# Graph sums and experts on one core: where the weights' bf16 parts are cast, and which engine adds the rows' bias

## Chip, cores and metric

One Trainium2 chip, one core of it. The metric is the device time of one execution in microseconds (us). Before the change: 493.82 us, the median of 3 runs (492.48 to 494.44).

## The reference, cut to what matters

There are 2048 nodes with 256 features each, 67,584 edges whose list is sorted by `dst`, and 8 experts.

```python
x = x + segment_sum(edge_weight[:, None] * layernorm(x)[dst], src) + node_vec1   # graph step
x = x + moe(layernorm(x)[None])                                                  # top 2 of 8 experts, gelu
```

`node_vec1` has one value per node, so it is a bias of the rows of x. The change lies in the graph step. The experts' part (router, lists of rows, slots of 256 rows that run two matmul layers) is untouched.

## The kernel before, in words

**Stage 1, the graph step**, takes the first 200 us or so. The sparse matrix of edge weights is built as dense column blocks and multiplied with the normalised x, called `xn_sb` (128 rows of nodes per partition block, 16 blocks b; 256 features and 8 router columns each). The result is added onto `acc`, which holds x from the start.

The matrix is built in 32 steps n (L472 on, `NH = 2 * NB`). One step makes 64 columns:

- For every fourth step a quarter q of the column pairs is prepared: GpSimd (POOL) gathers a run of `dst` (`get_run`, L215), ScalarE (ACT) counts how many lie before (`count_before`, L227, a Sign activation with a sum), VectorE (DVE) turns the count into a place (`get_at`), and POOL gathers windows of 128 edges (`get_win`, L240: source, destination, weight). `keys_of` (DVE, L271 to L275) makes keys of them. `turn_keys` transposes keys and weights on TensorE (PE, L283 and L284) and ACT casts them (L288, L291).
- Weights are fp32, and one-hots are multiplied in bf16. So each weight is split in three bf16 parts: part 0 is cast in `turn_keys`, parts 1 and 2 in `next_part(q, 1)` and `next_part(q, 2)`. Each subtracts the part before from the rest on DVE (L302) and casts the new rest on ACT (L303) into `w2`.
- `make_hots(n)` makes on DVE the one-hots `hl` (L313, 128x4096 bf16) and `eq` (L318), and multiplies `eq` with the weight parts into `hr`: parts 0 and 1 on DVE (L325, 128x2048), part 2 on POOL (L325, 128x1024). POOL's product is made to wait for DVE's. `ahead` and `between` are calls that are issued in between. The constant `iota_t` that `hl` and `eq` compare with lies in PSUM.
- `make_cols(n)` multiplies `hr` with `hl` on PE (L348, 96 matmuls). ACT copies the sums out of PSUM (L351), SP writes them to DRAM (`ad`, L352) and reads the step before back as columns (`ac`, L359).
- From n = 8 on, `dense` (PE, L366) multiplies finished column blocks with `xn_sb` for two row blocks at a time, in groups of 3, 3, 3, 3 and 4 column blocks; `add` (DVE) adds the sum onto `acc` one step later. The list `late` holds what is still to add.

The order of every engine is written out by hand (`tc.manual_schedule`), so an instruction that waits holds back all behind it on its engine. In each step the order is: hots of n + 1, gathers, late adds, columns of n, sums, keys turned, and then the `if n < ...` blocks.

**What the change touches.** Step 0 is prepared ahead of the loop. Its `make_hots(0, ...)` has `ahead=part_1`, which issues `next_part(0, 1)` and then `keep_x(3)`. `keep_x(i)` is an ACT copy of 128x1024 fp32 (L413) that takes the fourth transposed quarter of x (`turn_x(3)`, PE, L406) out of PSUM. `next_part(0, 2)` follows between `eq` and `hr`. So on ACT the order is: cast of part 1, copy of x, cast of part 2, then `sd` (Sqrt, L459) and `count_before(2)` (L227). `scale_x` (DVE, L465 and L466, `rs` and `shift` of 128x16) needs `sd`.

The first group of sums (8 adds, two row blocks each) also adds the bias: `add(..., first=True)` runs two `scalar_tensor_tensor` (L376, 128x256, PSUM + bias + acc) and one small `tensor_add` for the router columns (L378). All later adds are one `tensor_add` of 128x528 (L373).

Of the kernel before, what the change touches and what calls it, by code (L numbers as in the profile page):

```python
# [13 lines left out]
AF = mybir.ActivationFunctionType  # L14
OP = mybir.AluOpType
# [11 lines left out]
def kernel(  # L27
# [30 lines left out]
    nc = tc.nc  # L58
    N, D = x.shape
    NE, _, H = W1.shape  # L60
    E = src.shape[0]
    NB = N // P
# [18 lines left out]
    DX = D + NE  # L81
# [20 lines left out]
    acc = consts.tile([P, NB, DX], F32, name="acc")  # L102
# [110 lines left out]
    def get_run(q):  # L213
        runs[q] = find.tile([P, EJ], I32, name="run", bufs=3)
        nc.gpsimd.indirect_dma_start(  # L215
            out=runs[q],
            out_offset=None,
            in_=dst.rearrange("(p j) -> p j", p=P),
            in_offset=bass.IndirectOffsetOnAxis(ap=blk_i[:, q:q + 1], axis=0),
        )  # L220
# [4 lines left out]
    def count_before(q):  # L225
        sign = find.tile([P, EJ], BF16, name="sign")
        nc.scalar.activation(sign, runs[q], AF.Sign, bias=colp[:, q:q + 1], scale=-1.0,  # L227
                             accum_out=at[:, q:q + 1])
# [69 lines left out]
    def next_part(q, i):  # L298

        k2, w2, rest = parts[q]  # L300
        r = prep.tile([P, P], F32, name=f"r{i}")
        nc.vector.tensor_tensor(by_half(r), by_half(rest), w2[:, :, i - 1, :, 0], OP.subtract)  # L302
        nc.scalar.copy(w2[:, :, i], by_half(r)[..., None].to_broadcast([P, P // GH, GH, 2]))  # L303
        parts[q] = (k2, w2, r)

    def make_hots(n, *between, ahead=None):

        k2, w2, _ = parts[n // 4]  # L310
        g = n % 4
        hl = hotl.tile([P, GH, P], BF16, name="hl")
        nc.vector.tensor_tensor(hl.rearrange("p g (n t) -> p g n t", t=2),  # L313
                                two(k2[:, 0], g, P), pair(P), OP.is_equal)
        if ahead:
            ahead()
        eq = hotr.tile([P, GH, RK], BF16, name="eq")
        nc.vector.tensor_tensor(eq.rearrange("p g (n t) -> p g n t", t=2),  # L318
                                two(k2[:, 1], g, RK), pair(RK), OP.is_equal)
        for b in between:  # L320
            b()
        hr = hotr.tile([P, 3, GH, RK], BF16, name="hr")

        def times(engine, i0, i1):
            return engine.tensor_tensor(  # L325
                hr[:, i0:i1].rearrange("p i g (n t) -> p (i g) n t", t=2),
                eq[:, None, :, :].to_broadcast([P, i1 - i0, GH, RK]),
                w2[:, g, i0:i1].rearrange("p i g t -> p (i g) t")[:, :, None, :]
                .to_broadcast([P, (i1 - i0) * GH, RK // 2, 2]), OP.mult)

        v = times(nc.vector, 0, 2)
        third = times(nc.gpsimd, 2, 3)
        tc.add_manual_dep(third.ins, v.ins.name, WAITS, reason="beside one-hots of rows")
        return hl, hr
# [26 lines left out]
    def dense(cbs, b):  # L361

        pa = ps_s.tile([P, 2, 512], F32, name="py1")
        for i in range(2):
            for c in cbs:
                nc.tensor.matmul(pa[:, i, :DX], acs[c][:, b + i, :], xn_sb[:, c, :],  # L366
                                 start=(c == cbs[0]), stop=(c == cbs[-1]))
        return b, pa, cbs[0] == 0

    def add(b, pa, first=False):  # L370

        if not first:
            nc.vector.tensor_add(acc[:, b:b + 2, :], acc[:, b:b + 2, :], pa[:, :, :DX])  # L373
            return
        for i in range(2):
            nc.vector.scalar_tensor_tensor(acc[:, b + i, :D], pa[:, i, :D], nv_c[:, b + i:b + i + 1],  # L376
                                           acc[:, b + i, :D], op0=OP.add, op1=OP.add)
        nc.vector.tensor_add(acc[:, b:b + 2, D:], acc[:, b:b + 2, D:], pa[:, :, D:DX])  # L378

    ads, acs = {}, {}  # L380
    ET = mybir.EngineType
# [1 line left out]
    with tc.manual_schedule(engines=ALL):  # L383
        first = find.tile([P, 1], F32, name="first")
# [25 lines left out]
        def keep_x(i):  # L410
            pt = xTs[i]
            xTs[i] = rowsp.tile([P, GH // QP, P], F32, name="ar")
            nc.scalar.copy(xTs[i], pt)  # L413
# [17 lines left out]
        for _ in range(3):  # L431
            get_win(0)
        nc.vector.scalar_tensor_tensor(wc, ws[:, None, :].to_broadcast([P, KD, NE]), -1.0 / D,
                                       wr_sb, op0=OP.mult, op1=OP.add)
# [13 lines left out]
        weigh_x(1)  # L448
        turn_x(3)

        def part_1():
            next_part(0, 1)
            keep_x(3)

        hots = {0: make_hots(0, lambda: next_part(0, 2), ahead=part_1)}
        get_run(3)
        block_stats(bn, mv, acc, range(15, NB))
        sd = small.tile([P, NB], F32, name="sd", bufs=1)
        nc.scalar.activation(sd, mv[:, :, 1], AF.Sqrt, bias=eps_sb, scale=1.0)  # L459
        count_before(2)  # L460
        rs = small.tile([P, NB], F32, name="rs", bufs=1)
        shift = small.tile([P, NB], F32, name="shift", bufs=1)

# [8 lines left out]
        for n in range(NH):  # L472
# [30 lines left out]
            for p in late:  # L503
                add(*p)
# [6 lines left out]
            while len(todo) > NB // 2 and (budget >= len(todo[0][0]) or n == NH - 1):  # L511
                cbs, b = todo.pop(0)
                budget -= len(cbs)
                if len(late) == 2:
                    add(*late.pop(0))
                late.append(dense(cbs, b))
# [9 lines left out]
            if n < 4:  # L526
                for b in range(4 * n, 4 * n + 4):
                    nc.scalar.activation(xn_sb[:, b, :D], acc[:, b, :D], AF.Identity,
                                         bias=shift[:, b:b + 1], scale=rs[:, b:b + 1])
            if n == 1:  # L530

                tr = ps_a.tile([P, 4, P], F32, name="pa").rearrange("p a b -> p (a b)")
                nt = NE * KH + 2 * NE * KD + NB
                cols = consts.tile([P, nt], F32, name="cols")
                o = 0
                for rows in (b1_rows, g_rows, be_rows, nv_rows):
                    m = rows.shape[0]
                    nc.tensor.transpose(tr[:, o:o + m], rows, ident[:m, :m])
                    o += m
                nc.scalar.copy(cols, tr[:, :nt])  # L540
                nv_c = cols[:, NE * (KH + 2 * KD):]
# [8 lines left out]
            if n == 8:  # L550
# [3 lines left out]
                                               op1=OP.subtract)  # L554
# [12 lines left out]
        for p in late:  # L567
            add(*p)
# [9 lines left out]
    with tc.If(n_used < E):  # L578
        nc.sync.dma_start(xn_d.rearrange("(b p) d -> p b d", p=P), xn_sb)
        nc.sync.dma_start(acc[:, :, :D], xv)  # L580
        for b in range(NB):
            nc.vector.tensor_scalar(acc[:, b, :D], acc[:, b, :D], nv_c[:, b:b + 1], None,
                                    op0=OP.add)
# [6 lines left out]
        with tc.tile_pool(name="any", bufs=2) as anyp, tc.tile_pool(  # L590
# [5 lines left out]
            with tc.For_i(0, E // P, 1) as t:  # L596
# [18 lines left out]
                for b in range(NB):  # L615
                    hot = anyp.tile([P, P], F32, name="hot")
                    nc.vector.tensor_scalar(hot, iota_p, s_b[:, b:b + 1], w_t, op0=OP.is_equal,
                                            op1=OP.mult)
# [53 lines left out]
    with tc.manual_schedule(engines=ALL - {ET.Pool}):  # L672
# [526 lines left out]
        for p in range(2):  # L1199
            late.append(dense(groups[-1], 2 * p))  # L1200

        def finish(p, more=True):

            add(*late.pop(0))
            if more and p + 2 < NP:
                late.append(dense(groups[-1], 2 * p + 4))
            square(2 * p)
            square(2 * p + 1)
# [148 lines left out]
```

## Time and profile before

| | |
|---|---|
| median of 3 runs | 493.82 us (492.48 to 494.44) |
| the profiled execution, its own time | 489.82 us |
| its span, first to last instruction | 488.1 us |
| granted TensorE clock, mean | 0.958 |
| busy, share of the span | PE 92%, PEld 78%, DVE 57%, ACT 37%, POOL 39% |
| ACT `L413` copy of 128x1024 | 0.99 to 1.01 us |
| ACT `L303` cast of a weight part | 0.41 us |
| ACT `L528` scaling of 128x256, four in a row | 2.06 to 2.08 us |
| DVE `L376` with two instructions, then `L378` | 0.87 us, 0.16 us |
| DVE `L373` | 0.70 us |

How to read it: busy PE time is that of pipelined matmuls whose ends are modelled. A row of the timeline has start and duration in us, engine, line, operation, what it writes and reads, and in brackets the idle time of its engine before it and what ended it. An instruction on DVE or ACT can start some 0.1 us before the one ahead has ended, so the pace of a chain is read from start to start.

### The profile page before, as it was taken

Reading aid. Unit: us, or ns where it says so; the run is one execution under the profiler, and the core shown is the slowest. Engines: PE = TensorE matmul, PEld = TensorE weight load, DVE = VectorE, ACT = ScalarE, POOL = GpSimd, SP = SyncE. Lnnn points to the kernel's source line nnn. Section 1 sums busy time; section 2 is a strip of 40 time slices with the busy share of each in tenths; the row PEclk is TensorE's granted clock in tenths of the full one; section 3 lists DMA queues with packets and bytes.
Section 4 is the critical chain, followed back from the end, with each engine's and each line's share of the span. In section 5 each row is a group of like instructions: output and inputs, shape, how many; then the busy total and the mean of one; then the engine's idle time right before and its main releaser. Section 6 shows DMA issues by size and latency. Waiting matters only on the chain. (4 is left out here: it accounts for less than half of the span.)

```text
span 488.1 us, 12137 instructions
## 1 busy us (share of the span) xinstructions
PE 447.8 (92%) x4972; PEld 379.7 (78%) x4972; DVE 276.6 (57%) x643; ACT 178.6 (37%) x408; POOL 191.1 (39%) x157
## 2 busy tenths in 40 slices
PE   4876588999999989899999999999999999999992
PEld 3765466887887878788888888888877778888882
DVE  7999999999999972217849322321434231221111
ACT  2476734243242210027483433223331333322330
POOL 3577674455543430000132644333452333622331
PEclk9575879999999999999999999999999999999998
DMA  7228999989799599933532898998897747822520
GB/s 222 55 79 214 263 274 284 254 210 248 185 230 240 133 239 263 361 124 109 179 105 45 260 355 239 348 343 259 280 351 226 240 116 217 220 60 47 175 73 23
DMA packets 83252, 99.38 MB, mean 204 GB/s; under 512 B 8800, under 2 KB 73872, under 8 KB 81072
## 3 DMA queue, kind: packets, MB, share of 16 engines
q1 hardware_dynamic: 74000, 84.03, 58.0%
q0 software_dynamic: 7712, 13.38, 12.2%
q10 hardware_dynamic: 1472, 1.06, 0.7%
q8 instruction: 43, 0.70, 0.6%
q14 instruction: 25, 0.20, 0.1%
HBM read 72.61 MB, written 27.94 MB: 206 GB/s over the span
## 5 line engine op out<-in xcount | busy, mean ns | idle before, releaser
L366 PE MATMUL py<-xn_sb,ac 128*128 128x264 f32 x512 | 122.0, 394 | 2.7 <-DVEq L578 1.4
L1047 PE MATMUL ph<-xeT,w 128*128 128x256 f32 x512 | 114.7, 381 | 1.7 <-PEq L1304 1.0
L1061 PE MATMUL py<-w,hT 128*128 128x256 f32 x512 | 114.3, 381 | 0.0
L366 PEld LDWEIGHTS py<-xn_sb,ac 128*128 128x128 f32 x512 | 95.8, 191 | 21.3 <-issue 4.1
L1047 PEld LDWEIGHTS ph<-xeT,w 128*128 128x128 f32 x512 | 96.8, 190 | 16.2 <-issue 1.7
L1061 PEld LDWEIGHTS py<-w,hT 128*128 128x128 f32 x512 | 96.0, 190 | 13.0 <-issue 0.8
L1049 ACT ACTIVATE hT<-ph,ec 128x256 f32<-128x256 f32 x128 | 60.4, 473 | 106.0 <-PE ph L1047 55.9
L325 POOL TENSOR_TENSOR hr<-eq,w 128x1024 bf16<-128x1024 bf16 x32 | 61.2, 1912 | 73.5 <-DVE hr L325 58.9
L1069 POOL DMA_INDIRECT y_d<-ys,to_i x28 | 45.3, 1619 | 89.9 <-DVE ys L1064 56.1
L313 DVE TENSOR_TENSOR hl<-k,iota_t 128x4096 bf16<-128x4096 bf16 x32 | 72.9, 2279 | 0.0
L348 PE MATMUL pa<-hl,hr 128*32 128x128 bf16 x3072 | 58.0, 234 | 15.3 <-POOL hr L325 8.4
L348 PEld LDWEIGHTS <-hr 128*32 128x32 bf16 x3072 | 49.0, 104 | 27.0 <-issue 12.8
L973 POOL DMA_INDIRECT xs<-xr_d,to_i x36 | 37.5, 1043 | 67.3 <-DVE z L712 40.1
L351 ACT COPY ar<-pa 128x512 f32<-128x512 f32 x64 | 36.4, 583 | 49.0 <-PE pa L348 42.3
L1021 DVE TENSOR_SCALAR xeT<-px,ec 128x256 f32<-128x256 f32 x34 | 16.9, 539 | 64.7 <-PE px L1012 63.9
L1064 DVE SCALAR_TENSOR_TENSOR ys<-py,wt,b2w 128x256 f32<-128x256 f32 x32 | 15.3, 484 | 64.6 <-PE py L1061 48.9
L325 DVE TENSOR_TENSOR hr<-eq,w 128x2048 bf16<-128x2048 bf16 x32 | 39.1, 1223 | 0.6
L373 DVE TENSOR_TENSOR acc<-acc,py 128x528 f32<-128x528 f32 x32 | 22.2, 700 | 28.7 <-PE py L366 28.7
L1036 ACT ACTIVATE b2w<-b,wt 128x256 f32<-128x256 f32 x34 | 15.3, 499 | 33.5 <-DVE wt L1034 31.3
L318 DVE TENSOR_TENSOR eq<-k,iota_t 128x1024 bf16<-128x1024 bf16 x32 | 21.8, 681 | 0.0
L680 ACT ACTIVATE sq<-acc,less_m 128x256 f32<-128x256 f32 x16 | 8.0, 498 | 32.7 <-DVE acc L373 32.7
L303 ACT CAST w<-r 128x256 bf16<-128x256 f32 x16 | 6.5, 404 | 29.1 <-DVE r L302 29.0
(236 smaller groups left out, 325.1 us busy)
## 6 DMA issues: line engine op xcount, KB each, us to landing
w<-in_L_ffn_W SPq DMA_DIRECT2D x38, 1024.0 KB, 9.3
ad<-ar SPq DMA_DIRECT2D x64, 256.0 KB, 4.1
ac<-ad SPq DMA_DIRECT2D x32, 512.0 KB, 5.8
b<-in_L_ffn_b SPq DMA_DIRECT2D x19, 128.0 KB
out<-y_d SPq DMA_DIRECT2D x4, 512.0 KB, 5.2
xr_d<-rec SPq DMA_DIRECT2D x1, 1300.0 KB, 5.5
y_d<-acc SPq DMA_DIRECT2D x1, 1280.0 KB
acc<-in_x SPq DMA_DIRECT2D x2, 512.0 KB, 5.0
```

The source lines that it names most:

```text
L313: nc.vector.tensor_tensor(hl.rearrange("p g (n t) -> p g n t", t=2), two(k2[:, 0], g, P), pair(P), OP.is_equal)
L318: nc.vector.tensor_tensor(eq.rearrange("p g (n t) -> p g n t", t=2), two(k2[:, 1], g, RK), pair(RK), OP.is_equal)
L325: return engine.tensor_tensor(hr[:, i0:i1].rearrange("p i g (n t) -> p (i g) n t", t=2), eq[:, None, :, :].to_broadcast([P, i1 - i0, GH, RK]),
L348: nc.tensor.matmul(pa[j * RK:(j + 1) * RK, m, :], hr[:, i, g, :], hl[:, g, :], start=(i == 0), stop=(i == 2), tile_position=(0, j * RK))
L351: nc.scalar.copy(ar[:, m0:m0 + 4, :], pa)
L366: nc.tensor.matmul(pa[:, i, :DX], acs[c][:, b + i, :], xn_sb[:, c, :], start=(c == cbs[0]), stop=(c == cbs[-1]))
L373: nc.vector.tensor_add(acc[:, b:b + 2, :], acc[:, b:b + 2, :], pa[:, :, :DX])
L973: nc.gpsimd.indirect_dma_start(out=(sets[s.set][0] if into is None else into)[:, t, :], out_offset=None, in_=(xr_d if rows is None else ro ...
L1047: nc.tensor.matmul(ph, w1[:, k, c * P:(c + 1) * P], xeT[:, k, :], start=(k == 0), stop=(k == KD - 1))
L1049: nc.scalar.activation(hT[:, c, :s.n * P], ph, AF.Gelu, bias=ec[:, c:c + 1], scale=1.0)
L1061: nc.tensor.matmul(py, hT[:, c, t * P:(t + 1) * P], w2[:, c, :], start=(c == 0), stop=(c == KH - 1))
L1069: st = nc.gpsimd.indirect_dma_start(out=y_d[:, :], out_offset=bass.IndirectOffsetOnAxis(ap=tos[s.to][:, t:t + 1], axis=0), in_=ys, in_offs ...
```

## The change: what it does

1. The copy of the fourth quarter of x (`keep_x(3)`) goes from between the two casts of step 0 to behind `count_before(2)`. On ACT the order becomes: cast of part 1, cast of part 2, `sd`, `count_before(2)`, copy of x.
2. `add` is one `tensor_add` of 128x528 for every group. The bias is added by ACT in place on `acc`, two Identity activations of 128x256 at the end of each of the steps 4 to 11 (row blocks 0 and 1 in step 4, up to 14 and 15 in step 11). The sums of row blocks 0 and 1 begin in step 8.

DVE has 8 fewer entries (16 + 8 instructions become 8), ACT has 16 more instructions; the orders of PE, POOL and SP are unchanged.

```diff
-    def add(b, pa, first=False):
-
-        if not first:
-            nc.vector.tensor_add(acc[:, b:b + 2, :], acc[:, b:b + 2, :], pa[:, :, :DX])
-            return
-        for i in range(2):
-            nc.vector.scalar_tensor_tensor(acc[:, b + i, :D], pa[:, i, :D], nv_c[:, b + i:b + i + 1],
-                                           acc[:, b + i, :D], op0=OP.add, op1=OP.add)
-        nc.vector.tensor_add(acc[:, b:b + 2, D:], acc[:, b:b + 2, D:], pa[:, :, D:DX])
+    def add(b, pa):
+        nc.vector.tensor_add(acc[:, b:b + 2, :], acc[:, b:b + 2, :], pa[:, :, :DX])
+
+    def add_bias(b):
+
+        nc.scalar.activation(acc[:, b, :D], acc[:, b, :D], AF.Identity, bias=nv_c[:, b:b + 1],
+                             scale=1.0)
...
-        def part_1():
-            next_part(0, 1)
-            keep_x(3)
-
-        hots = {0: make_hots(0, lambda: next_part(0, 2), ahead=part_1)}
+        hots = {0: make_hots(0, lambda: next_part(0, 2), ahead=lambda: next_part(0, 1))}
         get_run(3)
         block_stats(bn, mv, acc, range(15, NB))
         sd = small.tile([P, NB], F32, name="sd", bufs=1)
         nc.scalar.activation(sd, mv[:, :, 1], AF.Sqrt, bias=eps_sb, scale=1.0)
         count_before(2)
+
+        keep_x(3)
...
                     nc.scalar.activation(xn_sb[:, b, :D], acc[:, b, :D], AF.Identity,
                                          bias=shift[:, b:b + 1], scale=rs[:, b:b + 1])
+            elif n < 4 + NB // 2:
+                for b in range(2 * (n - 4), 2 * (n - 4) + 2):
+                    add_bias(b)
```

More of the change, by code (lines that the diff above doesn't have):

```diff
@@ L367, in dense @@
                                  start=(c == cbs[0]), stop=(c == cbs[-1]))
-        return b, pa, cbs[0] == 0
-    def add(b, pa, first=False):
-        if not first:
-            nc.vector.tensor_add(acc[:, b:b + 2, :], acc[:, b:b + 2, :], pa[:, :, :DX])
-            return
-        for i in range(2):
-            nc.vector.scalar_tensor_tensor(acc[:, b + i, :D], pa[:, i, :D], nv_c[:, b + i:b + i + 1],
-                                           acc[:, b + i, :D], op0=OP.add, op1=OP.add)
-        nc.vector.tensor_add(acc[:, b:b + 2, D:], acc[:, b:b + 2, D:], pa[:, :, D:DX])
+        return b, pa
+    def add(b, pa):
[3 more added lines that the diff above has]
+                             scale=1.0)
     ads, acs = {}, {}
```

## Prediction

> **What bounds the kernel now.** I read the slices of the page first, then the timeline of each engine over the steps that the change touches, then who waited for whom there, and last the experts' part. The slices, twelve microseconds each, give the stage its bound:
>
> ```profile
> DVE  7999999999999972217849322321434231221111
> ACT  2476734243242210027483433223331333322330
> ```
>
> DVE is full from 18 to 180 us, ACT is not. DVE's timeline shows no wait in that stretch but 0.1 us ahead of L465 (26.06), 0.76 ahead of an L376 (70.81) and 1.79 at 176.03. So in these steps a microsecond less on DVE is one less to the end, as long as PE keeps up. Behind it, from 186 to the end, PE waits about 3 us in all by its list of waits: it is the bound there, and starts when the graph step lets it. So a gain of the graph step should reach the end whole.
>
> The start of step 0, in the timeline of all engines (start, duration, what ended the idle time):
>
> ```profile
> 21.42 1.22 DVE L325 TENSOR_TENSOR hr<-eq,w 128x2048 bf16<-128x2048 bf16 x1
> 24.50 1.01 ACT L413 COPY ar<-py 128x1024 f32<-128x1024 f32 x1 [3.36 <-PE py L406]
> 25.41 0.41 ACT L303 CAST w<-r 128x256 bf16<-128x256 f32 x1
> 25.90 1.91 POOL L325 TENSOR_TENSOR hr<-eq,w 128x1024 bf16<-128x1024 bf16 x1 [5.14 <-ACT w L303]
> 26.34 1.50 DVE L466 SCALAR_TENSOR_TENSOR shift<-mv,rs 128x16 f32<-128x16 f32 x1
> 27.77 0.21 DVE L271 TENSOR_SCALAR b_i<-win_s 128x128 int32<-128x128 int32 x1
> ...
> 65.76 0.17 DVE L553 SCALAR_TENSOR_TENSOR less_m<-mv,cols 128x16 f32<-128x16 f32 x1
> ```
>
> Read it as a chain: ACT waits 3.36 us for x's transposes, so the second cast comes at 25.41, so POOL's product at 25.90. Then `shift`, a tiny instruction, lasts 1.50 us and ends with POOL's product (27.81). The same form on the same shape took 0.17 at 65.76 with POOL idle. Both read two tensors of SBUF; so `shift` was held by the product.
>
> The adds, DVE's timeline:
>
> ```profile
> 81.98 0.87 DVE L376 SCALAR_TENSOR_TENSOR acc<-py,cols,acc 128x256 f32<-128x256 f32 x2
> 82.76 0.16 DVE L378 TENSOR_TENSOR acc<-acc,py 128x16 f32<-128x16 f32 x1
> 82.84 2.28 DVE L313 TENSOR_TENSOR hl<-k,iota_t 128x4096 bf16<-128x4096 bf16 x1
> ...
> 108.84 0.70 DVE L373 TENSOR_TENSOR acc<-acc,py 128x528 f32<-128x528 f32 x1
> 109.45 2.28 DVE L313 TENSOR_TENSOR hl<-k,iota_t 128x4096 bf16<-128x4096 bf16 x1
> ```
>
> From start to start an add with bias holds DVE 0.86 us, a plain one 0.61.
>
> **Part 1, the cast ahead of the copy.** The rest for part 2 is ready at 21.50 (L302, 21.22 + 0.28), and ACT is free from 21.15. The cast runs 21.55 to 21.96, and POOL's product no longer waits for it but for DVE's L325, which ends at 22.64: it runs about 22.7 to 24.6 instead of 25.9 to 27.8. `sd` needs the last block statistics (DVE, 23.19) and is done by 23.5 instead of 26.03. DVE then goes on from L318 (25.28) at its usual pace of 0.60 to an independent instruction: `rs` at 25.88, `shift` at 26.13, L271 some 0.1 later at about 26.2 instead of 27.77. From L271 to the next L325 other steps take 1.24 to 1.29 us (37.35 to 38.64, 55.27 to 56.51), here 1.32. **So DVE gains 1.6 us**: L325 starts at about 27.5, not 29.09.
>
> What is moved past: the copy of x stands behind `count_before(2)`, whose run POOL issued at 19.82; it had landed by 25.93, where the Sign started. At the latest the Sign ends at 26.8 and the copy at 27.9. Behind the copy wait the copies of step 0's matrix sums, at 29.18 before; PE makes these from 24.4 on without the 3.07 us that it waited for POOL. So nothing behind is later than before. `get_run(3)` on POOL goes from 27.96 to about 24.8, with nothing late behind it. SP and its DMAs follow the ACT copies.
>
> The unknown: the product now lies beside the last BATCH_NORM pair and `hl` on DVE, and no row shows batch statistics beside a product. If held until 24.6, DVE loses about 1.6 and the gain is nil; if not, nothing. Nearest rows: `rs`, one tensor from SBUF, took 0.25 beside the product, and a reduce of one tensor (L562, 174.09, beside the product of 173.73) took 0.15; `hl` took 2.25 without and 2.28 with it. I take 0. [...]
>
> **Part 2, the bias.** 8 adds of 0.86 become 0.61: 8 x 0.25 = 2.0 us off DVE. On ACT 16 activations come in. The nearest row is L528, same shape, same `acc`, 2.06 us for four: 1.03 a step for the steps 4 to 11. ACT is busy 8.36 of 14 us in 52 to 66 and 9.76 of 26 in 66 to 92, so there is room. At nothing I cost it because of this cover, at its tightest in step 5: the matrix copies of 53.35 would come 1.6 earlier and go back by 1.03, to 52.8; PE needs the buffer of the first for the second half of step 6, which it reaches some 1.1 after POOL's product (54.23 less 1.6), at 53.7, while the copy ends at 53.4. Without the cover it costs up to 1.03 in one step. The DMA write behind it stands in a backlog anyhow. In place on `acc` is not shown; the pair L294 and L295, the second in place, differ by 0.03.
>
> **Does PE keep up?** At 66 to 108 it hardly does, so the sum is made there. PE's waits from 62 to 182:
>
> ```profile
> PE pa L348 <- POOL hr L325: 3.0, 3, 1.7
> PE pa L348 <- issue: 1.8, 1, 1.8
> PE py L366 <- issue: 1.0, 1, 1.0
> PE py L366 <- DMA ac<-ad: 0.3, 1, 0.3
> ```
>
> The first sums (66.39) wait for the third column block, which lands at 68.7, and end at 70.78; DVE's first add waits for them 0.76. So DVE's lead gets past here only if the block lands earlier. Its read was issued at 63.20, when the write of step 5 had landed after some 8 us in a backlog that begins with the copies at 48.46; these follow a gather that landed at 44.0, 6.6 after POOL issued it at 37.36, behind a product that DVE paces. All of that moves by 1.6; I take 1.6 (bounds: 0.6, if the new ACT work holds the write of step 5 by its 1.03; 2.3, if DVE's wait goes too).
>
> From then PE works without a pause to 121.8, but for 1.8 us of "issue" in step 11 (80.6 to 82.4). The sums of step 11 end at 86.41, 0.49 ahead of their add (86.90). By then DVE would be 3 x 0.25 = 0.75 further than PE, so it waits 0.26 and keeps 0.49; with this add and the next two 1.24, cut to 0.92 by the second sums of step 13 (end 98.08, add at 99.00); with that add and the last **1.4 of the 2.0**. Later margins are wider (102.39 to 103.92, 107.05 to 108.84), and PE wins 1.4 by its waits for products at 121.80 (1.16), 151.57 (0.17) and two of 0.15 and 0.3 inside L348 (115.61, 146.56). So the wait at 176.03 and the last product move by as much.
>
> **Sum:** 1.6 + 1.4 = 3.0 us. Against the profiled execution's own 489.82 (span 488.1 and 1.7 around it) that is 486.8. The median of the runs lies 4.0 above that execution; I take the same loss from it: 493.82 - 3.0 = **490.8 us**.
>
> **The rivals.**
> - *PE's pause does not come again.* The 1.8 us has no releaser, a pause of supply by the look of it. Without it the margins of step 11 and 13 are 2.3 and more, and all 2.0 count: 3.6 off, 490.2; with the 0.7 of DVE's wait 4.3, 489.5. Against it: such pauses recur (1.0 at 178.47).
> - *The block lands late.* Lead past the first add 0.6, so 0.6 + 1.4 = 2.0: 491.8. For it speaks the DMA share of 1.04 at 52 to 66; against it, that step 5's write queues behind a read that moves anyway.
> - *The product holds the batch statistics*, and the change of casts does nothing for DVE: 1.4 off, 492.4. The rows of `rs` and L562 speak against it.
> - *PE falls behind on a lower clock*, the slower side. The granted clock was 0.70 at 20 to 62, and from 65.1 to 68.5 too it was halved: there four records of L366 took 2.07 us, where the next eight took 2.02. PE's order of idle times is moved by the change, so other stretches of 66 to 108 may be slow. Each 3.4 us at half clock costs PE 1.7; two such stretches eat the gain of 3.0, and four, 6.8, make it 3.8 slower: 497.6. It decides from the point where DVE's adds wait over 3 us in sum. Against it: L366 kept its 0.245 a record from 68.8 on.
>
> **Chances and range.** Forecast (2.5 to 3.5 off) 0.45; no pause 0.19; late landing 0.16; product holds 0.12; lower clock 0.05; something else, no gain, 0.03. Range 489.0 to 493.4: from the best case less 0.5 of run to run spread to the held product plus 1.0, the half width of the runs shown. A measurement can tell about 0.5%, 2.5 us. Faster by more: forecast 0.40 and no pause 0.19, 0.59. Within: the rest of the forecast, late landing, product, others, 0.36. Slower: 0.05.
>
> **What would show it.** POOL's first L325 at 22.7, not 25.9; the 128x16 `shift` at 0.2, not 1.5; the L325 of 29.09 at 27.5; adds all 0.70, 0.61 from start to start; the wait ahead of the first add still near 0.8; small waits of DVE for PE in steps 12 and 14; the last product at 177.4 instead of 180.40. A `shift` of 1.5, a BATCH_NORM pair of over 1 us, or a first add that waits over 1.5 would make the forecast wrong.

## The result and the profile after

Eleven runs of the changed kernel have a median of 489.03 us (486.59 to 491.17), eleven of the kernel before 492.58 (491.14 to 495.52). The ratio is 0.9922, with a 95% interval of 0.9900 to 0.9945: 0.78% faster, 3.8 us of 492.58. The profiled execution took 488.61 us, its span is 486.8 us and its mean granted clock 0.952.

The slices of the page after, DVE and ACT, twelve microseconds each:

```profile
DVE  7999979999999962227849332321433321221111
ACT  2576746343242220028482433233332333222330
```

DVE is as full as before up to 180 us, but for the 7 in the slice of 61 to 73 us. What was won lies inside the nines, and only the timeline shows it. The start of step 0 after the change, all engines:

```profile
21.64 0.41 ACT L303 CAST w<-r 128x256 bf16<-128x256 f32 x1 [0.40 <-DVE r L302]
22.66 0.42 DVE L250 BATCH_NORM_STATS2 bn<-acc 128x6 f32<-128x256 f32 x1
22.90 1.91 POOL L325 TENSOR_TENSOR hr<-eq,w 128x1024 bf16<-128x1024 bf16 x1 [2.04 <-DVE hr L325]
23.12 0.18 DVE L251 BATCH_NORM_AGGREGATE mv<-bn 128x2 f32<-128x6 f32 x1
...
26.27 0.18 DVE L462 SCALAR_TENSOR_TENSOR shift<-mv,rs 128x16 f32<-128x16 f32 x1
...
27.60 1.22 DVE L325 TENSOR_TENSOR hr<-eq,w 128x2048 bf16<-128x2048 bf16 x1
```

The cast comes at 21.64, POOL's product at 22.90 instead of 25.90, and `shift` (now L462) takes 0.18 instead of 1.50. The batch statistics beside the product are not held (0.42 and 0.18). DVE is at the next L325 1.49 us earlier. The adds (now L371), DVE's timeline:

```profile
71.52 0.70 DVE L371 TENSOR_TENSOR acc<-acc,py 128x528 f32<-128x528 f32 x1 [2.95 <-PE py L366]
...
82.18 0.70 DVE L371 TENSOR_TENSOR acc<-acc,py 128x528 f32<-128x528 f32 x1
82.80 2.28 DVE L313 TENSOR_TENSOR hl<-k,iota_t 128x4096 bf16<-128x4096 bf16 x1
```

Each add holds DVE for 0.62 us, as forecast. But the first waits 2.95 us for its sums, where the profile of before showed 0.76: without these waits the last L325 would be 3.5 us earlier (179.00 less 0.76, to 177.68 less 2.95), with them 1.3, as the spans are (488.1 to 486.8). The medians show more (3.55), so at least one of the two waits is likely to be unusual. That is the question of the experiments.

### The profile page after: what moved, and what is told of

Same layout as the page of the kernel before. It is cut to its first block, busy times and chain, and to the rows that moved or that the text cites. A ratio compares the mean times of both kernels' runs of the same rounds, so it can differ in the third digit from the quotient of the medians.

```text
span 486.8 us, 12135 instructions
## 1 busy us (share of the span) xinstructions
PE 452.7 (93%) x4972; PEld 383.2 (79%) x4972; DVE 273.0 (56%) x627; ACT 185.1 (38%) x424; POOL 191.1 (39%) x157
## 5 line engine op out<-in xcount | busy, mean ns | idle before, releaser
L366 PE MATMUL py<-xn_sb,ac 128*128 128x264 f32 x512 | 122.9, 395 | 3.9 <-issue 2.5
L366 PEld LDWEIGHTS py<-xn_sb,ac 128*128 128x128 f32 x512 | 96.1, 192 | 22.7 <-issue 4.9
L325 POOL TENSOR_TENSOR hr<-eq,w 128x1024 bf16<-128x1024 bf16 x32 | 61.2, 1912 | 72.0 <-DVE hr L325 58.2
L348 PE MATMUL pa<-hl,hr 128*32 128x128 bf16 x3072 | 60.1, 235 | 11.5 <-issue 4.4
L348 PEld LDWEIGHTS <-hr 128*32 128x32 bf16 x3072 | 50.3, 104 | 24.4 <-issue 16.4
L371 DVE TENSOR_TENSOR acc<-acc,py 128x528 f32<-128x528 f32 x40 | 27.8, 700 | 31.7 <-PE py L366 31.7
L325 DVE TENSOR_TENSOR hr<-eq,w 128x2048 bf16<-128x2048 bf16 x32 | 39.1, 1223 | 0.6
```

The lines of the kernel that those rows point to most:

```text
L325: return engine.tensor_tensor(hr[:, i0:i1].rearrange("p i g (n t) -> p (i g) n t", t=2), eq[:, None, :, :].to_broadcast([P, i1 - i0, GH, RK]),
L348: nc.tensor.matmul(pa[j * RK:(j + 1) * RK, m, :], hr[:, i, g, :], hl[:, g, :], start=(i == 0), stop=(i == 2), tile_position=(0, j * RK))
```

## The experiments

A number that recurs is the wait ahead of the first add, as a profile shows it. "L325(1)" and "L325(31)" are the starts of DVE's part of the product in the rows of steps 1 and 31 (29.09 and 179.00 before); "between" is their distance less the wait of the first add; the two kernels that add later (experiment 2) have another order there and are left out; "pauses" is the sum of PE's idle times named issue (the profile shows nothing that PE waited for) from 44 to 75 us. All times in us, one profiled execution each.

| kernel | order of casts | adds | L325(1) | wait | L325(31) | between | span | pauses |
|---|---|---|---|---|---|---|---|---|
| before | old | old | 29.09 | 0.76 | 179.00 | 149.15 | 488.1 | 0 |
| before, second profile | old | old | 29.41 | 3.75 | 183.03 | 149.87 | 492.5 | 6.88 |
| before, third profile | old | old | 29.58 | 1.92 | 180.77 | 149.27 | 490.4 | 8.64 |
| bias alone | old | new | 29.44 | 3.64 | 180.49 | 147.41 | 491.0 | 8.93 |
| casts alone | new | old | 27.61 | 0 | 176.83 | 149.22 | 487.0 | 0 |
| after | new | new | 27.60 | 2.95 | 177.68 | 147.13 | 486.8 | 5.39 |
| after, second profile | new | new | 27.59 | 0.28 | 175.01 | 147.14 | 484.3 | 1.07 |
| no bias | new | new | 27.63 | 0 | 175.78 | 148.15 | 485.2 | 0.79 |
| x weighed early | old | old | 29.47 | 0 | 179.02 | 149.55 | 488.2 | 2.80 |
| casts, DVE held | new | old | 29.24 | 2.06 | 180.41 | 149.11 | 489.5 | 7.39 |
| shift later | old | old | 29.25 | 3.21 | 181.79 | 149.33 | 491.3 | 6.84 |
| blocks moved | old | old | 29.31 | 4.90 | 183.19 | 148.98 | 492.4 | 2.63 |

**1. The two parts by themselves, the whole again, and without ACT's new work.** Casts alone is the kernel before with this edit:

```diff
-        def part_1():
-            next_part(0, 1)
-            keep_x(3)
-        hots = {0: make_hots(0, lambda: next_part(0, 2), ahead=part_1)}
+        hots = {0: make_hots(0, lambda: next_part(0, 2), ahead=lambda: next_part(0, 1))}
...
         count_before(2)
+        keep_x(3)
```

> Only the order of the casts is changed; the bias stays on DVE. If DVE's lead of 1.6 us passes the first add (theory of the prediction), 1.6 us less than before, and a profile in which shift takes 0.2 us. If the lead is lost at the first add, because the sums that it waits for are pinned by PE and the column read (rival, as the profile of the changed kernel has it: a wait of 2.95 us there), 0 to 0.5 us less, with a wait at the first add longer than 0.76 by 1.6.

Measured: median 489.42 us against 492.39 for before, ratio 0.9949 (0.9919 to 0.9979), which is 2.5 us (1.0 to 4.0). The first add does not wait at all in this profile, so the rival fails, and the gain is rather over the 1.6 of the theory.

Bias alone is the changed kernel with that edit undone.

> Only the bias is moved to ACT; the order of the casts is the old one, so shift takes 1.5 us again. Theory: 1.4 to 2.0 us less than before (8 adds of 0.25, cut where PE is just behind). Rival, that ACT's 16 new instructions hold PE's buffers or the column writes in steps 4 to 7: under 1 us less, and a longer wait at the first add.

Measured: 492.78 us, ratio 0.9983 (0.9955 to 1.0011), 0.8 us with an interval that holds nothing and 2.2. Both signs of the rival are there, a small gain and a longer wait (3.64), but not its cause: the read of step 5's column block was issued at 63.30, as in the three profiles of before (63.00 to 63.94), and the waits of before without any new work of ACT are as long (experiment 2).

The changed kernel once more:

> The changed kernel once more, for a second profile. If the wait of 2.95 us at the first add is a thing of that one execution, it will be shorter or longer by 1 us or more here and the median 3 to 4 us less than before. If it belongs to the change, it will be 2.5 to 3.4 us again.

Measured: 487.46 us, ratio 0.9904 (0.9870 to 0.9938), 4.7 us. The wait was 0.28, so the 2.95 belongs to that one execution.

No bias is the changed kernel with the body of that loop gone:

```diff
                 for b in range(2 * (n - 4), 2 * (n - 4) + 2):
-                    add_bias(b)
+                    pass
```

> The changed kernel with the bias left out altogether (neither DVE nor ACT adds it, so the output lacks node_vec1). It tells what ACT's 16 activations cost: as forecast nothing, so the same time as the changed kernel within 0.5 us; if they delay the copies of steps 4 to 7, 0.5 to 1 us less than the changed kernel.

Measured: 487.31 us, ratio 0.9898 (0.9859 to 0.9937). Beside 0.9904 with the activations, these cost nothing that can be measured. But each interval is 1.7 to 1.9 us wide to either side, more than the 0.5 to 1 us that this run was to tell apart, so a cost of that size is not excluded. The block of step 5 was issued at 58.27 here, and with the activations at 58.72 and 60.17 (second profile and first). A pair of them took 0.89 to 0.94 us in the profile after.

What follows: the distance "between" is 148.98 to 149.87 with the old adds, whatever the casts, and 147.13 to 147.41 with the new adds. So the adds give DVE about 2.0 us, all of the 8 x 0.25. (No bias has 148.15, with two short waits of DVE for PE, 0.30 and 0.34, in it.) The casts give 1.5 to 2.0 us at L325(1). And yet the bias alone hardly shows in the time. The first add, in the timelines of bias alone and then of casts alone:

```profile
74.25 0.70 DVE L371 TENSOR_TENSOR acc<-acc,py 128x528 f32<-128x528 f32 x1 [3.64 <-PE py L366]
```

```profile
68.66 0.88 DVE L376 SCALAR_TENSOR_TENSOR acc<-py,cols,acc 128x256 f32<-128x256 f32 x2
```

In these two profiles the order of the casts sets not only when DVE starts but also whether PE has the first sums ready. With one profile of each this could be the spread between executions, so it is tried in 2 and 4.

**2. Is the 0.76 us of before typical? And can the wait be passed by?** First, the kernel before as it is:

> The kernel before, once more, for a second profile. Theory: shift 1.5 us again, L325 of step 1 at 29.1 to 29.5, and a wait at the first add that differs from 0.76 by over 1 us, with a span longer than 488.1 by about that difference. Rival: a wait of 0.5 to 1 again with a span that differs for another reason.

Measured: 494.31 us, span 492.5; L325(1) at 29.41, only 0.3 later than in the first profile, but a wait of 3.75 us at the first add (74.34). DVE's timeline:

```profile
74.34 0.87 DVE L376 SCALAR_TENSOR_TENSOR acc<-py,cols,acc 128x256 f32<-128x256 f32 x2 [3.75 <-PE py L366]
```

The profile that the forecast read was one of the better executions of its kernel (489.82 us, where 22 other runs of it gave 489.32 to 495.38).

Then the first add is put 2.9 us later in DVE's order, in both kernels:

```diff
+            if n == 10:
+                also.insert(0, lambda: add(*late.pop(0)))
...
-            for p in late:
-                add(*p)
-            late = []
+            if n != 9:
+                for p in late:
+                    add(*p)
+                late = []
```

> The kernel before, with the add of the first sums put 2.9 us later in DVE's order (behind the next hl and eq), so that DVE has work while it waits for them. Theory: the wait at the first add varies between executions (0.76 and 3.64 us in two profiles with the old order of casts) and is about 3 us in most runs of the kernel before; then this is 2 to 3 us less than before, and its runs lie closer together. Rival: the profiled wait of 0.76 is the usual one and the runs differ for another reason; then 0.5 to 0.8 us less at most, with the same spread.

> The changed kernel with the same edit. Theory: with the new order of casts the first sums come earlier (waits of 2.95, 0.28, 0 and 0 us in four profiles), so less is left to win here: 0.5 to 2 us less than the changed kernel, 5 to 6 less than before. Against the other kernel of this edit, where no wait at the first add is left in either, the change is worth its work on DVE alone: 1.5 + 2.0 = 3.5 us. Rival, that PE is the bound there: a difference of 1.4 us or less between the two.

Measured: the kernel before with this edit 491.09 us, ratio 0.9972 (0.9948 to 0.9996), with no wait at the first add (73.41) but 1.38 us at the next (78.32). That is 1.4 us (0.2 to 2.6), less than the 2 to 3 expected, and its runs lie no closer together (488.87 to 493.06). The changed kernel with it 486.23, ratio 0.9895 (0.9864 to 0.9925), the lowest median of this study, though its interval overlaps that of the changed kernel. The two medians differ by 4.9 us, where DVE's work alone gives 3.5, and the 1.38 that one of them still waits is most of the rest. So the wait is part of what runs lose, and a later place for the add wins some of it back with the old casts.

**3. Was `shift` held, or slow in itself?** In the kernel before, `scale_x` goes behind the keys of the next window:

```diff
-                also += [scale_x, lambda: f.append((1, keys_of(1))), lambda: get_at(2)]
+                also += [lambda: f.append((1, keys_of(1))), scale_x, lambda: get_at(2)]
```

> The kernel before, with shift put behind the keys of the next quarter in DVE's order. If a DVE instruction with two inputs in SBUF is held by POOL's product, the instruction that now comes first, f (L273, two inputs), takes the 1.2 to 1.5 us and ends at about 27.8, and shift takes 0.2; L325 of step 1 stays within 0.4 us of 29.1. Rival, that shift itself is slow, for example because its input comes from ACT: shift takes 1.5 us still, and f 0.3.

Measured: 493.04 us, span 491.3. DVE's timeline (POOL's product ran from 26.10 to 28.03):

```profile
26.30 1.88 DVE L273 SCALAR_TENSOR_TENSOR f<-b_i,win_s 128x128 f32<-128x128 int32 x1
28.10 0.28 DVE L274 SCALAR_TENSOR_TENSOR f<-win_d,b_i 128x128 f32<-128x128 int32 x1
28.90 0.17 DVE L466 SCALAR_TENSOR_TENSOR shift<-mv,rs 128x16 f32<-128x16 f32 x1
```

Now another instruction with two tensors from SBUF lies beside the product, and it is the one that is held: 1.88 us against 0.28 for the same form right after. `shift` takes 0.17. That a DVE instruction with two tensors from SBUF is held by POOL's product is shown for these two instructions, and L325(1) is as late as before (29.25).

**4. Why is PE late?** With the old casts PE waits 3.07 us in step 0 for POOL's product, here in the first profile of before:

```profile
27.87 2.54 PE L348 MATMUL pa<-hl,hr 128*32 128x128 bf16 x88 [3.07 <-POOL hr L325]
```

In x weighed early, the casts stay as before, and PE does a later piece of work in that pause:

```diff
+            if n == 0:
+                weigh_x(2)
             make_cols(n, *hots.pop(n))
...
-            if n < 2:
-                weigh_x(2 + n)
+            if n == 1:
+                weigh_x(3)
```

> The kernel before with one thing moved: the first weighing of x that stands in step 0 (16 products of L419, x's third quarter) is done ahead of step 0's matrix sums on PE, in the 3.07 us in which PE waits for POOL's product, and no longer behind them. The order of the casts stays as in the kernel before. Theory (the second gain of part 1 is PE's: its pause of 3 us goes, so the matrix copies of steps 1 to 3, and behind them the column block of step 5, come 2 to 4 us earlier and the first add no longer waits): shift still about 1.5, L325 of step 1 still at 29.1 to 29.4, the read of the third column block issued about 60 instead of 63, the wait ahead of the first add under 1 us where three of four profiles with the old order of casts showed 3.2 to 3.75; the product of step 31 at 178.0 to 179.5, span 487 to 489, the time 0.2 to 0.6 per cent under the kernel before. Rival (the block comes earlier because DVE and POOL start the steps earlier, PE's pause is hidden): the wait stays at 3 to 3.75, the product of step 31 at 181 to 183, the same time as the kernel before within 0.2 per cent.

Measured: 491.31 us against 492.13, ratio 0.9972 (0.9949 to 0.9994). PE's and DVE's timelines:

```profile
24.63 3.42 PE L419 MATMUL pa<-wc,ar 128*128 128x8 f32 x16
27.98 3.16 PE L348 MATMUL pa<-hl,hr 128*32 128x128 bf16 x96
```

```profile
26.72 1.50 DVE L466 SCALAR_TENSOR_TENSOR shift<-mv,rs 128x16 f32<-128x16 f32 x1
...
70.38 0.88 DVE L376 SCALAR_TENSOR_TENSOR acc<-py,cols,acc 128x256 f32<-128x256 f32 x2
```

`shift` is held as ever, L325(1) is at 29.47, and still the first add has no wait; the column block of step 5 was issued at 60.24 instead of 63.0 to 63.94 (three profiles of before). The theory's numbers came out. (L325(1) is a little over the 29.4 named.) In time it is 1.4 us (0.3 to 2.5). PE's lead is a gain by itself, apart from DVE's.

The counterpart keeps the new casts and gives back DVE's 1.5 us with a reduce that nothing reads:

```diff
             nc.vector.scalar_tensor_tensor(shift, mv[:, :, 0], -1.0, rs, op0=OP.mult, op1=OP.mult)
+            pad = small.tile([P, 5], F32, name="pad", bufs=1)
+            nc.vector.tensor_reduce(pad, acc[:, 0:5, :D], AX.X, OP.add)
```

> The kernel with the new order of casts and the old adds, and on DVE a reduce of 128x1280 behind shift, about 1.4 us of work whose result nothing reads: it gives back what DVE wins at shift, and leaves what POOL and PE win. Theory (the two gains are apart): shift 0.2, the reduce 1.3 to 1.5, L325 of step 1 at about 29.0 as in the kernel before; the pause of 3 us of PE in step 0 gone, the third column block's read issued 58 to 61, the wait ahead of the first add under 1 us; the product of step 31 at about 178.3 (176.83 of the kernel with casts alone, plus 1.5), span about 488.5; 0.3 per cent slower than with the casts alone, and 0 to 0.4 per cent under the kernel before. Rival (all of part 1's gain is DVE's): the wait ahead of the first add comes back to 3 or more, and the time is that of the kernel before.

Measured: 491.35 us, ratio 0.9988 (0.9964 to 1.0012), 0.6 us with an interval that holds nothing; a wait of 2.06, the block's read at 61.93 (58 to 61 expected), L325(31) at 180.41 (178.3). Neither the theory (under 1) nor the rival (3 or more): the pause of 3.07 was gone, but PE then waited 0.98 for `f`, which the reduce delays, and had 7.39 us of pauses later. So the two gains are not cleanly apart: PE needs DVE's start too, and how much of part 1 is DVE's and how much PE's stays open.

The kernel before a third time:

> The kernel before once more, one look, for how far the wait ahead of its first add differs between executions. Theory: the wait is a matter of PE's speed in steps 0 to 2; where the 96 products of step 1 (L348) take about 2.75 us it is 3 to 4 us and the span 491 to 493; where they take about 1.5 it is under 1 and the span 488 to 489. Rival (the wait has nothing to do with it): some other pairing of the two.

Measured: 492.18 us, span 490.4, wait 1.92. The theory's pairing missed: step 1's 96 products took 3.75 us with their pauses (33.28 to 37.03), slower than in the second profile (2.75), and the wait was shorter. PE's speed in that step is not what decides. The column of pauses does better: up to 2.80 us go with waits of 0 to 0.76, 5.39 and more with 1.92 to 3.75. (The exception, blocks moved, is below.)

**5. What are PE's pauses?** In the second profile of before, PE's timeline:

```profile
51.98 0.74 PE L348 MATMUL pa<-hl,hr 128*32 128x128 bf16 x40 [1.23 <-issue]
53.44 2.45 PE L348 MATMUL pa<-hl,hr 128*32 128x128 bf16 x88 [0.71 <-ACT ar L351]
57.63 1.68 PE L348 MATMUL pa<-hl,hr 128*32 128x128 bf16 x56 [1.75 <-issue]
59.25 0.69 PE L283 MATMUL pa<-ident,f 128*128 128x128 f32 x2
59.73 0.42 PE L284 MATMUL pa<-ident,win_w 128*128 128x128 f32 x1
60.08 2.22 PE L348 MATMUL pa<-hl,hr 128*32 128x128 bf16 x69
64.09 3.39 PE L348 MATMUL pa<-hl,hr 128*32 128x128 bf16 x123 [1.79 <-issue]
```

Count the products between the pauses: 40 + 88 = 128, and 56 + 2 + 1 + 69 = 128. Each has a weight load (842 products and 842 loads from 20 to 62 us of the first profile of before), so they lie 256 instructions apart. (The next pause, in the first sums, comes 123 + 3 = 126 products later, four instructions short; this is not explained.) Bias alone and after have their long pauses at the same places of the program; some shorter ones (0.16 and 0.47 in after) lie elsewhere and stay unexplained. The instruction queue of the DMA moves 16 KB packets (43 in the second profile, 0.70 MB). That looks like PE waiting for its program, which is a reading so far. To tell this from a buffer or a transfer, 64 instructions are put ahead, in idle stretches of PE:

```diff
+        for _ in range(16):
+            nc.tensor.transpose(xp[:16, 1, :16], ident[:16, :16], ident[:16, :16])
         weigh_x(0)
```

(and 16 more, into the tile of `ws`, ahead of L397).

> The kernel before with 32 transposes of 16x16 put into two early idle stretches of PE (16 ahead of L397, 16 ahead of the first L419), whose results nothing reads. In four profiles that wait long at the first add, PE's pauses without a releaser (named issue) come at the same places of its program, 128 products with their 128 weight loads apart: after the 200th product L348 counted from the start of step 3, after the 328th, after 69 products behind the transposes L283 and L284 of step 7, and 3 products L366 into the first sums. Theory (PE waits there for the next block of its own program, and a block holds 256 instructions): 64 instructions put ahead of them move every such pause by 32 products forward, to the 168th and the 296th product of L348, to 37 products behind those transposes, and to 27 products ahead of the end of step 8. Rival (the pauses belong to the data or to the time, a buffer or a transfer that the trace does not name): they stay at the 200th, the 328th, 69 behind the transposes, and inside the first sums. Shift 1.5 as in the kernel before; span 488 to 493. In an execution in which PE is early enough there are no such pauses, and nothing is told apart.

Measured: span 492.4. PE's timeline from step 7 on:

```profile
58.44 0.29 PE L348 MATMUL pa<-hl,hr 128*32 128x128 bf16 x8
60.01 0.62 PE L348 MATMUL pa<-hl,hr 128*32 128x128 bf16 x29 [1.27 <-POOL hr L325]
60.82 1.45 PE L348 MATMUL pa<-hl,hr 128*32 128x128 bf16 x67 [0.19 <-issue]
64.05 1.22 PE L348 MATMUL pa<-hl,hr 128*32 128x128 bf16 x61 [1.79 <-POOL hr L325]
67.72 0.94 PE L348 MATMUL pa<-hl,hr 128*32 128x128 bf16 x27 [2.44 <-issue]
```

The pauses now come after 8 + 29 = 37 products and 67 + 61 = 128 later, 27 ahead of the end of step 8: the places that the theory named. (The second of these lay 3 products into the first sums before, so it moved by 30 and not 32.) At the 168th and the 296th product this execution had none. So the long pauses belong to places of PE's program and not to the data.

The packets of the instruction queue lie close to the pauses. In the profile after three of 16 KB end at 54.14, 59.67 and 66.34, and PE goes on at 55.65, 61.29 and 67.63, which is 1.51, 1.62 and 1.29 us later. In the first profile of before two end at 80.94 and 176.94, and PE goes on at 82.37 and 178.47, 1.43 and 1.53 us later. Other packets have no pause behind them (65.43 and 73.99 in before). That PE waits for what such a packet brings is the author's reading; no run shows what a packet holds.

Blocks moved also shows that they are not the whole of the wait: with 2.63 us of them the first add waited 4.90, because the last one lay right ahead of the first sums, which then ran at half their speed (8 of 12 rows in 3.86 us, where 8 took 2.02 in before) and waited 0.48 for the column block. Nor need the last pause alone be the wait in the others: in the second profile of before and in bias alone the block's read was issued at 63.00 and 63.30. The reads of the first profile of before took 5.4 to 7.0 us to land (63.20 to 68.6 and 57.39 to 64.4). With that, an estimate, the block was there between 68.4 and 70.0 and between 68.7 and 70.3, where the pauses ran from 68.34 to 70.45 and from 66.86 to 70.66. So without the pause PE would have waited 0.1 to 1.7 us for the block in the one and 1.8 to 3.4 in the other.

Why PE pauses at these places in some executions and not in others is not shown. Casts alone, without a pause from 44 to 75 us, waits for POOL's product there (1.79, 1.79 and 1.68 us); the second profile of before, with 6.88 us of pauses, has no such wait there. No run here tries whether the one goes with the other.

## Why the prediction was right or wrong

**Part 1 on DVE: right.** POOL's product at 22.90 (22.7 forecast), `shift` 0.18, L325(1) at 27.60 (27.5), 1.49 us won of the 1.6. That `shift` had been held by POOL's product agrees with experiment 3, where `f` in its place took 1.88 and `shift` 0.17.

**The product beside the batch statistics: right at nothing.** They took 0.42 and 0.18 beside it, as much as in before without it (22.56 and 23.01, the product at 25.90).

**ACT's 16 activations at nothing: not contradicted.** No bias 0.9898, with them 0.9904; a cost of under 1 us would not show in these runs.

**"I take 1.6" for the column block, and a wait that stays near 0.8: the step that failed.** The sum counts part 1 as a lead of DVE alone, which passes the first add as far as the column block comes earlier. The read of the block of step 5 was issued at 63.20 before, at 60.17 after and at 57.95 in casts alone, 3 to 5 us earlier:

```profile
63.20 0.45 SPq L359 DMA_DIRECT2D ac<-ad  x1
60.17 0.45 SPq L359 DMA_DIRECT2D ac<-ad  x1
57.95 0.45 SPq L359 DMA_DIRECT2D ac<-ad  x1
```

PE's pause of 3.07 us in step 0 goes with POOL's earlier product. The prediction named that pause, but used it only to show that nothing behind the copies gets later; it is a gain of its own, 1.4 us in experiment 4, that the sum put at nothing. Casts alone won 2.5 us (1.0 to 4.0). And the wait of 0.76 came from one execution: the others with the old casts and PE's old order have 1.92 to 4.90 (the add moved later left aside), those with the new casts and an undelayed DVE 0, 0, 0.28 and 2.95. So part 1 also takes most of a wait away that the forecast's profile hardly held. In the profile after, the 2.95 is no wait for the block either, but a pause of PE and sums at half their speed:

```profile
64.85 0.94 PE L366 MATMUL py<-xn_sb,ac 128*128 128x264 f32 x3
67.63 3.85 PE L366 MATMUL py<-xn_sb,ac 128*128 128x264 f32 x9 [1.85 <-issue]
```

**"1.4 of the 2.0" for part 2: too little.** The distance between the two L325 fell by 2.02 (149.15 to 147.13). The cut of 0.6 rested on the margins of one execution, with 1.8 us of issue in step 11. In the profile after this pause did not come. In its second profile it came as 0.40 (78.56), and DVE still lost nothing to it. In no bias it came as 1.54 (78.71), and there one of the small waits of DVE that were forecast shows, 0.30 at 95.59 (0.27 with the add moved later). So the margins differ from one execution to the next. The rival "PE's pause does not come again" has the sum that fits best (3.6 off, 490.2), but its reason holds in one of the two profiles. "The block lands late" is refuted by the second profile of after: its first add started at 68.73, when the sums with this block were done, and before the block itself landed only at 68.6 (63.20 + 5.4) and the add started at 70.81.

**The signs.** Of those named, a first add that waits over 1.5 should have made the forecast wrong: it did wait 2.95 in the profiled execution, and that pair of executions shows 1.2 us of gain (489.82 to 488.61) where 3.0 were forecast. The last product, POOL's of step 31, came at 179.07 instead of 180.40, where 177.4 was forecast, and DVE's part of it at 175.01 in the second profile (179.00 before). The sign holds for that pair and misleads for the medians, since before waited 3.75 and 1.92 in its other two profiles.

**The size.** Three runs of the changed kernel, as 493.82 was the median of three, have a median of 488.61, just under the stated range (489.0 to 493.4); eleven have 489.03, just inside. 3.0 us of 493.82 is a ratio of 0.9939, within the measured interval (0.9900 to 0.9945), at its upper end. Of the 1.8 us between 490.8 and 489.03, 1.2 is the base: before had 493.82 in three runs and 492.58 in eleven. The rest, 0.6, is the difference of the medians, 3.55, less the forecast 3.0. That DVE's two gains, 1.49 and 2.02, add up to nearly these 3.55 is in part luck: the wait at the first add, which is not in them, is 0.76 to 3.75 in the profiles of before and 0.28 to 2.95 in those of after.

**The lower clock as the slower side: it came, its sign did not.** The sums of L366 did run at half their speed in the profile after (nine rows in 3.85 us, 67.63), with a granted clock of 0.50 from 67.8 to 71.2, which is part of the 2.95. The kernel before has the same speed in its second profile (nine rows in 3.85 us, 70.45), so it is no cost of the change alone.

## What to carry to other kernels

When an engine's wait is removed, list everyone who waited for the same releaser: here POOL's late product held `shift` on DVE, which lay beside it (1.50 us against 0.17 and 0.18), and PE, which needed its result (3.07 us), and only the first was priced. Before a margin or a wait of under a few microseconds is carried from one profile into a sum, look at a second execution of the same kernel: it was 0.76 in one and 3.75 in the next. Where a profile names PE's pauses issue, count the instructions between two of them and move them by some that do nothing: here long ones lay 256 apart, and 64 instructions put ahead moved two by 32 and 30 products, so they belonged to places in the program and not to the data.

## What the runs showed of the hardware

- PE paused, with nothing named that it waited for, for up to 3.80 us (bias alone, 70.66), in some executions and not in others of one kernel: 0, 6.88 and 8.64 us from 44 to 75 in the three profiles of before. The places of three long pauses lay 128 products with their loads apart (40 + 88 and 56 + 2 + 1 + 69 in the second profile of before), and 64 instructions put ahead moved two places by 32 and 30 products. Five such pauses (0.69 to 2.22 us, three in after and two in before) ended 1.29 to 1.62 us after a 16 KB packet of the instruction queue.
- The same PE work takes two speeds from one execution to the next: 16 products of L419 1.85 or 3.42 us, 96 of L348 1.52 or 2.75 us, between 30 and 38 us of the first and the second profile of before. Where the clock was read, the slow speed goes with a granted clock of 0.50 and the fast one with 1.00: L419 3.42 us (before, 19.25) and 1.85 (before, 30.88), L348 2.75 (after, 38.64) and 1.52 (before, 32.66), L366 3.85 for nine (after, 67.63) and 2.02 for eight (before, 68.76).
- Two DVE instructions with two SBUF tensors that started during a POOL product ended with it or just after it: `shift`, 128x16, took 1.50 us and ended 0.03 us after it (before; 1.50 too in five other profiles in which it lies beside the product, 0.17 or 0.18 in the seven in which it does not), `f`, 128x128, took 1.88 (0.28 for the same form right after) and ended 0.15 after it. With one SBUF tensor, `rs` (0.25) and the batch statistics (0.42 and 0.18) were not held beside a product.
